# Layer 0 of a four-layer cross-attention kernel: transposed contexts by transfer, the first pair in three parts over two queues

## The chip, the core and the metric

The kernel runs on one core of a Trainium2 chip. The core has five engines with instruction streams of their own: PE (TensorE, matrix products and transposes), DVE (VectorE), ACT (ScalarE), POOL (GpSimd) and SP (SyncE, which here only issues transfers). Transfers between HBM and SBUF are carried out by 16 DMA engines; SP, ACT and POOL can issue them. The metric is the device time of one execution in microseconds (us), the median over runs.

## What is computed

The input is `x`, 16 batches of 56 tokens by 256 values, and a context `ctx_1024`, 16 batches of 1500 rows by 128 values. Four layers follow each other; each attends from the tokens of a batch to the 1500 context rows of that batch. The change touches only the first layer:

```python
def _L0_xattn_ref(hidden_states, memory, W_mem, W_gate, b_gate, norm_w):
    memory_proj = jnp.einsum('bme,de->bmd', memory, W_mem)
    scores = jnp.einsum('bnd,bmd->bnm', hidden_states, memory_proj) / jnp.sqrt(jnp.float32(D))
    attn = jax.nn.softmax(scores, axis=-1)
    memory_context = jnp.einsum('bnm,bmd->bnd', attn, memory_proj)
    gate_input = jnp.concatenate([hidden_states, memory_context], axis=-1)
    gate = jax.nn.sigmoid(jnp.einsum('bnf,df->bnd', gate_input, W_gate) + b_gate)
    fused = hidden_states + gate * memory_context
    return _rmsnorm(fused, norm_w)
```

The kernel multiplies the queries by `W_mem` first, so that scores and weighted sums are products with the context itself. Layers 1 and 3 are multi-head cross-attention with a feed-forward part, layer 2 is self-attention, cross-attention and a two-expert feed-forward part.

## The kernel before

**Tiling.** The 16 batches form four groups of four (`groups`, `gi`), and within a group two pairs, so that layer 0 runs over eight pairs, 0 to 7. The context of a batch is needed in two forms. For the weighted sums (line 610) its rows must lie on the partitions: `load_pair` (lines 506 to 518) brings it as a tile `kv` of 125 partitions by 12 x 128 values, 6144 bytes on each partition, 750 KB. For the scores (line 557) the 128 features must lie on the partitions: `turn_pair` (lines 520 to 538) makes a tile `kt` of 128 x 1500 by 12 PE transposes for each context (line 530), four into one PSUM tile, and a copy out of each PSUM tile, in turn by DVE (line 535) and ACT (line 536, recorded under line 245). The PSUM tiles of `turn()` come from a pool with two buffers. `scores_pair` (line 545) makes the scores of a pair in three columns of 500, both batches side by side, with the maxima by DVE (line 569) and the exponentials by ACT (line 576). All score products of a pair stand behind the pair's last transpose in PE's order.

**Order within layer 0.** `load_first` loads the first part of the weights, pairs 0 and 1 and the rest of the weights. `first0` turns pair 0 and makes its scores. Then `att0` runs for each group and each pair `at`: it loads pair `at + 2`, turns pair `at + 1` and makes its scores, and then transposes the weights of pair `at` (line 598) and makes its weighted sums (line 610). The hook `side()` at the head of a group finishes the group before (`post0`, lines 626 to 668) and prepares the next one (`pre0`: tokens `x` by a transfer, line 174; transposes, line 252; queries, line 498). A scheduler puts each engine's instructions into one fixed order when the kernel is built; each engine then follows its order, and an instruction that waits holds up all behind it. A transfer's issue stands in the order of its issuing engine and waits there until the tile that it fills is free.

**Buffers.** `kv` of pair n comes from the tag `kv`, `ot` or `hT` for n modulo 3 equal to 0, 1, 2, each with two buffers, so pair n + 3 reuses those of pair n and waits for pair n's weighted sums. The two `kt` of a pair come from the tags `kt` and `qa`, two buffers each.

**Queues.** The first context of a pair is loaded by SP, the second by POOL. SP's order over layer 0 is: the weights `w` (128 KB), `kv` of pairs 0 and 1, `w` (640 KB), `b_gate`, `norm_w`, the tokens of group 1, `kv` of pair 2, the tokens of groups 2 and 3, then loads for layer 1 that the scheduler put early (`Wq` 1024 KB, line 161; `WkT` and `Wv`, 512 KB each; a key mask `m32l` of 12 KB, line 143; `l2w` 256 KB; a second `Wq`), `kv` of pair 3, two more masks `m32l`, then `kv` of pairs 4 to 7. The masks have one buffer: each must have been expanded by POOL (line 147, to the tile `mkl`) before the next is loaded. POOL's order is: `kv` of pairs 0, 1 and 2, `mkl`, `kv` of pair 3, `mkl`, `kv` of pairs 4 to 7, each in its second context.

Of the kernel before, what the change touches and what calls it, by code (L numbers as in the profile page):

```python
# [9 lines left out]
F32 = mybir.dt.float32  # L10
# [10 lines left out]
B, N, M = 16, 56, 1500  # L21
D, DM = 256, 128
# [6 lines left out]
NS, SW = 3, 500  # L29
# [9 lines left out]
R = H * N  # L39
# [23 lines left out]
def tile_kernel(ctx: ExitStack, tc: tile.TileContext, a, layers=4, groups=NG):  # L63
# [3 lines left out]
    nc = tc.nc  # L67
# [3 lines left out]
    kpool = ctx.enter_context(tc.tile_pool(name="ctxp", bufs=2))  # L71
    mpool = ctx.enter_context(tc.tile_pool(name="mask", bufs=2))
    big = ctx.enter_context(tc.tile_pool(name="big", bufs=2))
# [19 lines left out]
    def turn():  # L93
        return psum(ps_t, "t")
# [149 lines left out]
    def scalar_copy(out, in_, scale=1.0):  # L244
        nc.scalar.activation(out, in_, AF.Copy, scale=scale)  # L245
# [159 lines left out]
    line, memory_w, halves_of, queries, heads_w, cross = {}, [], {}, {}, {}, {}  # L405
# [70 lines left out]
    def load_first():  # L476

        w = wpool.tile([128, 2048], F32, tag="w", name="w")
        memory_w.append(w)
        nc.sync.dma_start(w[:, :256], a["L0_w"][:, :256])  # L480
        load_pair(0)
        load_pair(1)
        nc.sync.dma_start(w[:, 256:1536], a["L0_w"][:, 256:])
        nc.sync.dma_start(w[:, 1536:1792], a["b_gate"].to_broadcast([128, D]))
        nc.sync.dma_start(w[:, 1792:], a["norm_w"].to_broadcast([128, D]))
# [19 lines left out]

    def load_pair(n):

        kvs = []
        for b, queue in ((2 * n, nc.sync), (2 * n + 1, nc.gpsimd)):

            if n % 3:
                kv = big.tile([128, 2 * R], F32, tag=("ot", "hT")[n % 3 - 1], name="kv_")
                kv = kv[:CP, : NC * DM].rearrange("p (c d) -> p c d", c=NC)
            else:
                kv = kpool.tile([CP, NC, DM], F32, tag="kv", name="kv")
            queue.dma_start(kv, a["ctx"][b])
            kvs.append(kv)
        halves_of[n] = kvs

    def turn_pair(n):  # L520
        kts = [
            kpool.tile([DM, M], F32, tag="kt", name="kt"),
            big.tile([128, 2 * R], F32, tag="qa", name="kt_")[:, :M],
        ]
        kvs = halves_of[n]
        for s in range(NS):
            for i in range(2):
                t = turn()
                for j in range(4):
                    last = nc.tensor.transpose(  # L530
                        t[:, j * CP : (j + 1) * CP], kvs[i][:, 4 * s + j, :], ident[:CP, :CP]
                    )
                dst = kts[i][:, s * SW : (s + 1) * SW]
                if (i + s) % 2:
                    nc.vector.tensor_copy(dst, t[:, :SW])
                else:
                    scalar_copy(dst, t[:, :SW])
        halves_of[n] = kts, kvs, last.ins.name

    def first0(gi, state):  # L540
        if not gi:
            turn_pair(0)
            scores_pair(0)
# [36 lines left out]
    def att0(gi, state, then, side, ends, last):  # L580
# [3 lines left out]
        for b0 in range(0, G, 2):  # L584
# [3 lines left out]
            if at + 2 < B // 2:  # L588
                load_pair(at + 2)
            if at + 1 < B // 2:  # L590
                turn_pair(at + 1)
                scores_pair(at + 1)
# [782 lines left out]
```

## Time and profile before

| | |
|---|---|
| median of 3 runs | 1768.75 us (1766.23, 1775.0, 1768.75) |
| profiled execution, its own time | 1774.53 us |
| span of the profiled execution | 1772.7 us, mean granted PE clock 0.986 |
| PE busy over the span | 1668.2 us (94%) |
| DVE, ACT, POOL busy | 1126.1, 1022.1, 112.1 us |
| moved by transfers | 106.80 MB, mean 60 GB/s |
| PE busy from 0 to 67 us | 35.9 us of 67 |
| PE busy from 67 to 165 us | 85.3 us of 98 |
| PE busy from 165 us to the end | 1547.0 us of 1607 |

The span is the time from the first to the last instruction of one profiled execution; the execution's own time is a little longer. Layer 0 takes up the first 170 us or so, where the work of layer 1 begins to mix in. In the tables of windows that follow, each row gives a stretch of the span, its length, the busy time of PE, of PE's weight loads, of DVE, ACT and POOL with their numbers of instructions, the granted clock, the mean busy share of the 16 DMA engines and what they moved in GB/s. In a timeline, a row gives the start, the length, the engine and line, and in brackets how long the engine sat idle before and what it waited for. `SPq` is the instruction stream of SP.

### The profile page before, as it was taken

What the parts mean: (1) busy time and instruction counts of PE and PEld (TensorE: products, weight loads), DVE (VectorE), ACT (ScalarE), POOL (GpSimd) and SP (SyncE); (2) the same over time, 40 slices, a digit from 0 to 9 for tenths busy, and PEclk for the clock granted to TensorE, in tenths of its full rate; (3) what the DMA queues carried; (4) which work ended last, traced back from release to release, by engine and by line L of the source; (5) the groups of instructions that cost most, each with busy time, mean ns of one, the idle gap of its engine ahead of it and who ended that gap; (6) DMA issues with size and microseconds to landing.
All of it is one profiled execution on the core that took longest, in us unless ns stands there. A gap on an engine that the chain in (4) does not pass through costs nothing.

```text
span 1772.7 us, 55493 instructions
## 1 busy us (share of the span) xinstructions
PE 1668.2 (94%) x23964; PEld 1104.3 (62%) x23964; DVE 1126.1 (64%) x2742; ACT 1022.1 (58%) x3580; POOL 112.1 (6%) x238
## 2 busy tenths in 40 slices
PE   4888999999999999999999999999999999999997
PEld 2566777776664556545665556556656777777765
DVE  2344866657765666777657776576488746666672
ACT  1443976757454446553755547457555876766663
POOL 0000000000011000110000000000000000000000
PEclk9999999999999999999999999999999999999998
DMA  6431203020030121000210002211200132212120
GB/s 175 126 109 45 77 24 108 25 89 25 14 133 28 43 97 46 21 20 20 99 69 20 20 20 99 74 38 43 99 21 16 48 119 64 76 52 89 44 68 8
DMA packets 60132, 106.80 MB, mean 60 GB/s; under 512 B 7430, under 2 KB 44950, under 8 KB 59878
## 3 DMA queue, kind: packets, MB, share of 16 engines
q1 hardware_dynamic: 58726, 97.01, 17.0%
q0 software_dynamic: 1152, 6.14, 1.4%
q8 instruction: 190, 3.11, 0.7%
q14 instruction: 64, 0.52, 0.1%
HBM read 102.23 MB, written 0.92 MB: 58 GB/s over the span
## 4 chain that ended last, share of the span: by engine, by line
PE 77%; DVE 12%; ACT 6%; DMA 3%; issue 2%; POOL 1%; SPq 0%; POOLq 0%; DVEq 0%
PE sc L339 21%; PE o L795 9%; PE mm L1166 4%; ACT p L381 4%; PE o L1133 4%; DVE p L392 4%; PE mm L858 3%; PE mm L846 3%; PE mm L831 3%; PE mm L682 3%; PE mm L1179 2%; PE t L702 2%; DVE p L344 2%; PE t L1055 2%; PE t L743 2%; PE t L751 2%
## 5 line engine op out<-in xcount | busy, mean ns | idle before, releaser
L381 ACT ACTIVATE p<-p,few 128x96 f32<-128x96 f32 (+1 forms) x1344 | 588.3, 440 | 3.8
L339 PE MATMUL sc<-kt,qa 128*32 128x375 f32 x3584 | 407.8, 486 | 5.1 <-issue 3.1
L392 DVE STREAM_TRANSPOSE p<-p 128x480 f32<-128x480 f32 (+3 forms) x319 | 316.5, 1003 | 53.0 <-ACT p L381 52.1
L344 DVE CUSTOM_DVE_ANT_0 p<-sc,no_mask 128x375 f32<-128x375 f32 x448 | 236.4, 536 | 95.1 <-PE sc L339 86.3
L381 ACT ACTIVATION_READ_ACCUMULATOR p<-p,few 128x1 f32 x1344 | 252.2, 188 | 0.0
L339 PE MATMUL sc<-ktl,qa 128*32 128x96 f32 x7168 | 200.1, 249 | 2.3 <-issue 1.6
L339 PEld LDWEIGHTS sc<-kt,qa 128*32 128x32 f32 x3584 | 126.8, 109 | 107.7 <-issue 70.1
L1133 PEld LDWEIGHTS o<-p,vc 128*32 128x32 f32 x6144 | 142.9, 110 | 75.8 <-issue 51.2
L339 PEld LDWEIGHTS sc<-ktl,qa 128*32 128x32 f32 x7168 | 157.7, 110 | 34.0 <-issue 17.3
L795 PE MATMUL o<-p,kvl 128*128 128x448 f32 x384 | 167.9, 565 | 1.2 <-DVE p L392 1.2
L1133 PE MATMUL o<-p,vc 128*32 128x64 f32 (+1 forms) x6144 | 159.7, 215 | 8.7 <-DVE p L392 7.1
L245 ACT ACTIVATE few<-t 128x14 f32<-128x14 f32 (+2 forms) x128 | 22.2, 174 | 212.7 <-PE t L373 212.7
L350 DVE TENSOR_TENSOR p<-sc,mkl 128x480 f32<-128x480 f32 (+1 forms) x192 | 113.6, 607 | 25.5 <-PE sc L339 25.3
L354 DVE TENSOR_REDUCE few<-p 128x5 f32<-128x480 f32 (+1 forms) x192 | 114.4, 612 | 2.8
L795 PEld LDWEIGHTS o<-p,kvl 128*128 128x128 f32 x384 | 67.0, 191 | 55.3 <-issue 44.7
L245 ACT ACTIVATE qa<-t 128x224 f32<-128x224 f32 (+1 forms) x96 | 38.4, 420 | 91.4 <-PE t L702 62.7
L1166 PE MATMUL mm<-xT,w 128*128 128x224 f32 (+1 forms) x384 | 81.0, 360 | 1.1 <-DVE h2T L1171 0.9
L1166 PEld LDWEIGHTS mm<-xT,w 128*128 128x128 f32 (+1 forms) x384 | 65.7, 178 | 15.6 <-DVE h2T L1171 5.3
L1055 PE MATMUL t<-l2w,kt 128*32 128x128 f32 x1536 | 60.2, 275 | 6.2 <-issue 5.8
L245 ACT ACTIVATE ot<-o 128x448 f32<-128x448 f32 x64 | 33.8, 527 | 54.0 <-PE o L795 54.0
L702 PE MATMUL t<-qT,wl 64*128 64x112 f32 x512 | 55.4, 284 | 3.2 <-DVE qa L713 2.0
L757 DVE TENSOR_TENSOR oT<-t,over 128x224 f32<-128x224 f32 x64 | 31.8, 551 | 41.3 <-PE t L751 38.2
(262 smaller groups left out, 2293.8 us busy)
## 6 DMA issues: line engine op xcount, KB each, us to landing
w<-in_L_W SPq DMA_DIRECT2D x16, 1024.0 KB
kt<-in_ctxT SPq DMA_DIRECT2D x16, 768.0 KB
w<-in_L_Wq SPq DMA_DIRECT2D x8, 1024.0 KB
w<-in_L_Wo SPq DMA_DIRECT2D x8, 1024.0 KB
ktl<-in_ctxT SPq DMA_DIRECT2D x32, 192.0 KB
kvl<-in_ctx_last SPq DMA_DIRECT2D x32, 192.0 KB
w<-in_L_v_qkv SPq DMA_DIRECT2D x4, 768.0 KB
w<-in_L_l_qkv SPq DMA_DIRECT2D x4, 768.0 KB
```

What stands on the lines that cost most here:

```text
L245: nc.scalar.activation(out, in_, AF.Copy, scale=scale)
L339: nc.tensor.matmul(sc[g * BW : (g + 1) * BW, at : at + w], q, k, start=True, stop=True, skip_group_check=True,)
L344: return nc.vector.tensor_tensor_reduce(u["p"][:, i, :w], sc[:, :w], u["mask"], 1.0, LOWEST, ALU.add, ALU.max, u["mx"][:, i : i + 1],).ins ...
L350: nc.vector.tensor_tensor(p, sc[:, : m * w].rearrange("p (i k) -> p i k", i=m), u["mask"].unsqueeze(1).to_broadcast([128, m, w]), ALU.add,)
L354: return nc.vector.tensor_reduce(u["mx"][:, i : i + m], p, AX.X, ALU.max).ins.name
L381: nc.scalar.activation(u["p"][:, i, : u["w"]], u["p"][:, i, : u["w"]], AF.Exp, bias=u["shift"][:, i : i + 1], accum_out=u["den"][:, i : i ...
L392: turned = nc.vector.transpose(blocks, blocks)
L702: nc.tensor.matmul(halves[e][:, j * TP : (j + 1) * TP], wkT[e * 64 : (e + 1) * 64, j0 + j, :], qT[e * 64 : (e + 1) * 64, j0 + j, tok], sta ...
L795: nc.tensor.matmul(o[:, : ub * BW], kv[:, j, :], p, start=start, stop=stop)
L1055: nc.tensor.matmul(p[g * BW : (g + 1) * BW, (j - j0) * DM : (j - j0 + 1) * DM], made["kt"][:, g, j * BW : (j + 1) * BW], cv, start=True, s ...
L1133: nc.tensor.matmul(o[cols, : pieces * BW], made["v"][:, j, cols], p.rearrange("p (i g) r -> p g i r", g=4)[:, g], start=start, stop=stop, ...
L1166: nc.tensor.matmul(p[:w, k * T : (k + 1) * T], wt[:, c, cols], xe[n][:, c, :], start=(c == 0), stop=(c == 1),)
```

## The change

For every pair but the first, the transposed tile of the pair's first context is loaded by SP from `ctxT`, an array with the transposed contexts that the kernel already has in HBM for later layers (128 rows of 6000 bytes, 750 KB). Only the second context of such a pair is still turned by PE: 12 transposes and 3 copies where there were 24 and 6. The tiles `kt` are now allocated in `load_pair`. The `kv` tiles are all still loaded, since the weighted sums need them. The second context of pairs 0 and 1 is loaded by ACT in place of POOL. For pair 0, each of the two contexts is loaded in three transfers of four of its twelve blocks (125 rows of 2048 bytes each).

```diff
 def load_pair(n):
     kvs = []
-    for b, queue in ((2 * n, nc.sync), (2 * n + 1, nc.gpsimd)):
+    kts = [
+        kpool.tile([DM, M], F32, tag="kt", name="kt"),
+        big.tile([128, 2 * R], F32, tag="qa", name="kt_")[:, :M],
+    ]
+    other = nc.scalar if n < 2 else nc.gpsimd
+    for b, queue in ((2 * n, nc.sync), (2 * n + 1, other)):
...
-        queue.dma_start(kv, a["ctx"][b])
+        for s in range(1 if n else NS):
+            cols = slice(None) if n else slice(4 * s, 4 * s + 4)
+            queue.dma_start(kv[:, cols], a["ctx"][b][:, cols])
         kvs.append(kv)
-    halves_of[n] = kvs
+    if n:
+        nc.sync.dma_start(kts[0], a["ctxT"][2 * n])
+    halves_of[n] = kts, kvs
 
 def turn_pair(n):
-    kts = [
-        kpool.tile([DM, M], F32, tag="kt", name="kt"),
-        big.tile([128, 2 * R], F32, tag="qa", name="kt_")[:, :M],
-    ]
-    kvs = halves_of[n]
+    kts, kvs = halves_of[n]
     for s in range(NS):
-        for i in range(2):
+        for i in range(1 if n else 0, 2):
```

## The prediction, made before the changed kernel ran

> **What bounds the kernel now.** I read the table of windows first, to find where PE is idle; then the chain of work that ended last, for what ends that idle time; then the timelines of PE, SP and POOL. Over the whole span PE is busy 94%, and from 165 us on 1547.0 us of 1607 with the DMA engines 0.17 busy. The change works before that, where PE is not the only bound.
>
> ```profile
> core 0: us, PE busy (x) PEld busy (x) DVE busy (x) ACT busy (x) POOL busy (x), PEclk, DMA share, GB/s
> 10.00:20.00 10.00, 0.00 (x0) 0.00 (x0) 0.00 (x0) 0.28 (x1) 0.00 (x0) 1.00 1.01 212
> 25.00:30.00 5.00, 5.00 (x25) 3.97 (x25) 1.44 (x3) 1.76 (x3) 0.00 (x0) 1.00 0.32 129
> ...
> 60.00:65.00 5.00, 3.66 (x51) 2.86 (x47) 0.51 (x2) 2.18 (x4) 0.00 (x0) 1.00 0.33 114
> 75.00:79.00 4.00, 3.37 (x25) 2.69 (x25) 3.07 (x6) 1.80 (x5) 0.00 (x0) 1.00 0.32 128
> ```
>
> Two things stand here. While SP's and POOL's contexts move together (10 to 20 us) all 16 DMA engines are busy, at 212 GB/s, 13 GB/s each. When little but one of SP's 125-row contexts is left (the other three rows) the share is 0.32, that is five engines of 16, at 25 GB/s each, 125 GB/s together. So a context by SP occupies five engines for 768,000 bytes / 125 GB/s = 6.1 us; POOL's contexts spread wider. I call those the five engines; my estimate is that a transfer of 128 rows (the weights, `kt`) or by POOL puts 5/16 of its bytes on them: 1.9 us for 750 KB.
>
> ```profile
> 9.33 27.36 DMA x<-in_x
> ...
> 36.74 1.01 PE mm L252 x4
> ...
> 49.91 1.12 PE o L610 x16
> 51.02 15.85 DMA kv<-in_ctx
> ...
> 67.01 0.70 PE t L530 x3
> ```
>
> The chain: PE waits for the tokens of group 1, which land at 36.7 us behind the contexts, and then for the context of pair 3, which is issued when pair 0's sums free its buffer at 51.0 and lands at 67.0 (2.2 us of PE idle).
>
> ```profile
> 121.88 3.90 PE L530 MATMUL t<-ident,kv 125*128 125x125 f32 x24
> 125.72 0.63 PE L557 MATMUL sc<-kt,l 128*64 128x500 f32 x1
> ```
>
> Turning a pair costs PE 3.84 us before its scores.
>
> ```profile
> 52.83 0.26 POOL L147 TENSOR_SCALAR mkl<-m32l 128x96 bf16<-128x96 uint8 x1 [44.90 <-DMA m32l<-in_mask_last]
> 53.35 0.57 POOL L516 DMA_DIRECT2D kv<-in_ctx  x1 [0.25 <-issue]
> 67.13 0.26 POOL L147 TENSOR_SCALAR mkl<-m32l 128x96 bf16<-128x96 uint8 x1 [13.21 <-DMA m32l<-in_mask_last]
> 67.61 0.57 POOL L516 DMA_DIRECT2D kv__509<-in_ctx  x1 [0.22 <-issue]
> 88.32 0.52 POOL L516 DMA_DIRECT2D kv__621<-in_ctx  x1 [20.15 <-PE o L610]
> ```
>
> POOL's loads stand behind its mask expansions, and those wait for masks that come through SP's queue. Pair 4's load went out at 67.6, right after a mask; PE needed it only at 88.6.
>
> **The change, part by part.**
>
> *Removed:* 12 transposes and 3 copies for each of pairs 1 to 7. In pair 4 the groups of four transposes start at 88.63, 89.15, 89.90, 90.57, 91.32, 91.89 and the scores at 92.47. With three groups the scores start about 0.6 after 89.90, 2.0 earlier; the first copy is now DVE's (0.68) and no longer ACT's (0.59): 1.9 us a pair, on PE's path. The copies gone from DVE and ACT are off the path.
>
> *Pair 0 in parts, ACT in place of POOL.* Four issues on ACT at SP's 0.28 to 0.38 us are 1.4 us between ACT's 7.1 and its next instruction at 9.92: hidden. An issue can block on a full queue (SP's third context took 11.27 us to issue at 9.86); ACT would then be free near 20, and its first copy is not needed much before. The bytes are dearer. By POOL a context took 1.9 us of the five engines; by a 125-row transfer of ACT it should take 6.1, as SP's do. No row shows an ACT transfer. The other bound is POOL's 1.9 (the tokens, below, would then land at 7.0 + 23.2 + 8.6 x 4120/3370 = 40.7); I take 6.1, since shape and source are SP's.
>
> The Trainium skill speaks against this part: in "DMA: Bandwidth & Descriptors", section "Why a DMA increments its semaphore by 16 and not by 1", a transfer of SP or ACT runs on the largest number of engines up to 16 that divides the slowest dimension of both sides, which for 125 rows is 5, while a direct copy by POOL may use all 16. By that rule the sum stands as below, with the tokens at 45.3; without it, with 40.7.
>
> *The start.* Work of the five engines up to the tokens of group 1, at 25 GB/s each: `w` 0.3, four contexts 24.6, POOL's pair 2 1.9, `kt` of pair 1 (now ahead of the tokens) 1.9, 896 KB of weights 2.3, tokens 0.6: 31.6 us. Before it was 0.3 + 2 x 6.1 + 3 x 1.9 + 2.3 + 0.6 = 21.1, and took 29.7 (7.0 to 36.7), so 8.6 were lost to sharing with the other eleven. Those now carry 2620 KB and no longer 3370, so I take 8.6 x 2620/3370 = 6.7. Tokens at 7.0 + 31.6 + 6.7 = 45.3, 8.6 later. Bounds: no loss, 38.6; the old ratio 29.7/21.1 = 1.41 on all of it, 51.6. Pair 0's own last part lands no earlier than its context did (0.3 + 12.3 + 1.9 of work, times 1.41, from 7.0: 27, against 24.4), so the parts buy nothing: PE waits at the tokens anyway. After the tokens PE has their transposes (1.0), the rest of pair 1's scores (2.2), queries (1.0) and pair 0's sums (45.13 to 51.02, 5.9), little of it overlapped: 9.9. Pair 0's sums end at 55.2, 4.2 late.
>
> *Pair 3.* Pair 2 gives back 1.9: PE is ready for pair 3 at 64.83 + 2.3 = 67.1. POOL's context, now ahead of the mask in POOL's order, goes out at 55.2 and lands 11.7 later (the median of its rows), 66.9. SP's context is no longer needed for turning, so the old wait goes; but the late start has used it up. Net at this point: 0.1 late; after pair 3's turn 1.8 early.
>
> *The masks.* All of this part is an estimate from the ratios above. In the built order SP now has `kt` of pair 3 (waits for pair 1's scores), `Wq`, pair 3's context (waits for pair 0's sums), `WkT`, `Wv`, `kt` of pair 4, and only then the first mask; `l2w`, `Wq`, pair 4's context, and then the second. Work on the five from the tokens to the first mask: pair 2's context 6.1, `kt` 1.9, tokens 1.1, `kt` 1.9, `Wq` 2.6, pair 3 6.1 + 1.9, `WkT` and `Wv` 2.6, `kt` 1.9 = 26.1. Before, from the tokens to pair 3's context, 23.7 took 30.3 us, 1.28 times. So first mask 45.3 + 33.4 = 78.7 (it was there by 52.8), pair 4 out at 79.0, landed 7.3 later (its row) at 86.3; PE is ready at 88.63 - 1.8 = 86.8: just in time. To the second mask: `l2w` 0.7, `Wq` 2.6, pair 4 6.1 + 1.9 = 11.3, times 1.28 = 14.5: 93.2. Then pair 5 by POOL, 10.0 in its row: 103.5. PE is ready at 101.65 - 1.8 - 1.9 = 97.9 and waits 5.6 us, with the end of group 0 queued behind those transposes. Pairs 6 and 7 stand behind no mask and have a whole pair's time.
>
> *Sum:* at pair 5 +1.9, then three turns of 1.9: -3.8 us. Beyond 165 us PE is the bound and keeps it. Profiled execution 1774.53 - 3.8 = 1770.7 (span 1768.9). That execution lies 5.8 above the median of the runs shown, so the forecast for the median is 1768.75 - 3.8 = 1765.
>
> **Rivals.**
>
> *The transfers keep up* (30%). For it: over the windows from 60 to 140 us the DMA engines are only 0.31 busy. Against it: the five engines' queue has some 70 us of work before the second mask. If the second mask lands by 87, pair 5 does not wait: 0.1 - 5 x 1.9 = -9.4, 1759. If the start is no later either, pair 3 is turned at 62.9 in place of 67.0: -4.1 - 9.5 = -13.6, 1755.
>
> *Slower: the mask gate on POOL* (27%). With the start's ratio 1.41 on all of it: tokens 51.6, first mask 88.4, second mask 104.3, pair 5 landed at 114.6, 13.0 after its old start, less 5.7: +7.3, 1776. It decides once the second mask lands after 97 (101.65 + 5.7 - 10.3); each microsecond more is one on the end. For it: the first window shows 13 GB/s an engine whenever all are busy. Against it: there are fewer loads by POOL at the start.
>
> *The change doesn't do what it says:* the first pair is not earlier by the parts. That is in my sum, not a case apart.
>
> **How the numbers follow.** Forecast (43%): 1765, own range 1760 to 1773. A measurement of this kernel tells about 0.5%, 8.8 us, from no change. Faster by more: nearly all of the first rival, 0.28. Slower by more: rather over half of the second, whose ratio must reach 1.46, 0.16. Else 0.56. The range reaches into both rivals, 1755 to 1778.
>
> **What would show it.** Right: 12 transposes for pairs 1 to 7 and 1.9 us before the scores; DMA share near 0.32 for most of 18 to 40 us; PE idle until the tokens at 42 to 48; POOL's mask expansions near 79 and 93, each directly ahead of a context; a PE wait at pair 5's first transposes. Wrong: tokens by 40, or no wait at pair 5 (then faster), or ACT held for more than 15 us at its issues, or a wait at pairs 6 or 7, which I exclude.

## The result and the profile after

The changed kernel takes 1763.59 us, the median of six runs (1759.62 to 1765.84); the kernel before, in six runs beside it, 1770.88 us (1766.23 to 1775.0). The ratio is 0.9967, 95% interval 0.9949 to 0.9985: faster by 0.33%, some 6 us, less than the 0.5% that the prediction took for a clear difference.

| profiled execution | before | after |
|---|---|---|
| its own time, span | 1774.53, 1772.7 us | 1765.84, 1763.9 us |
| PE busy over the span | 1668.2 us | 1659.2 us |
| PE busy from 0 to 67 us, granted clock there | 35.9 us, 0.97 | 35.6 us, 0.95 |
| PE busy from 67 to 165 us | 85.3 us | 85.0 us |
| moved by transfers, of it by ACT's queue | 106.80 MB, none | 112.16 MB, 1.54 MB |
| first scores of pairs 3, 5, 7 | 78.81, 112.06, 144.48 us | 76.86, 106.91, 136.94 us |

(The added lines shift the numbers: the turning transposes are now line 537, the scores 564, the weighted sums 617, a context's load 525, a transposed context's 528.)

The windows of the changed kernel; behind the length come the busy times of PE, its weight loads, DVE, ACT and POOL, the granted PE clock, the DMA share, and GB/s:

```profile
10.00:20.00 10.00, 3.01 (x10) 2.36 (x11) 0.00 (x0) 0.41 (x2) 0.00 (x0) 1.00 0.53 142
13.00:16.00 3.00, 0.00 (x0) 0.00 (x0) 0.00 (x0) 0.00 (x0) 0.00 (x0) 1.00 0.30 115
...
44.00:49.00 5.00, 4.83 (x14) 2.36 (x16) 1.31 (x3) 0.13 (x1) 0.00 (x0) 0.50 0.37 131
```

Where all 16 engines were busy before (share 1.01 from 10 to 20 us), they are now half busy: from 13 to 16 us three queues have contexts under way (SP's, ACT's and the rest of POOL's, which lands at 16.6), and still the share is that of five engines of 16. With SP's and ACT's alone, from 16.6 to 18.7 us, it is 0.32. The last row shows something that the prediction did not have: PE at a granted clock of 0.50.

The chain of the changed kernel (start, length, what):

```profile
6.99 25.41 DMA kv<-in_ctx
...
32.80 11.33 DMA x<-in_x
...
44.17 1.01 PE mm L252 x4
...
57.47 12.18 DMA kv<-in_ctx
...
69.79 0.51 PE t L537 x3
```

Pair 0's third part lands at 32.4 us (its whole context did at 24.4), the tokens of group 1 at 44.1 (before: 36.7). The context of pair 3 goes out at 57.5 when pair 0's sums have freed its buffer, and PE turns it at 69.8, 2.8 us later than before.

PE's timeline in the changed kernel:

```profile
37.55 0.58 PE L564 MATMUL sc<-kt,l 128*64 128x500 f32 x1
...
44.17 1.01 PE L252 MATMUL mm<-ident,x 112*128 112x112 f32 x4 [2.57 <-DMA x<-in_x]
45.11 1.10 PE L564 MATMUL sc<-kt__155,l 128*64 128x500 f32 x1
...
99.58 0.49 PE L537 MATMUL t<-ident,kv__579 125*128 125x125 f32 x3
...
118.51 1.16 PE L537 MATMUL t<-ident,kv 125*128 125x125 f32 x8
119.87 0.65 PE L537 MATMUL t<-ident,kv 125*128 125x125 f32 x4 [0.20 <-DVE kt__716 L542]
120.44 0.63 PE L564 MATMUL sc<-kt,l 128*64 128x500 f32 x1
```

The same product of scores takes 0.58 us before the wait for the tokens and 1.10 behind it: that is the half clock. Pair 5 (99.58) has no wait in brackets. Pair 6 is turned in 1.93 us (118.51 to 120.44) and no longer in 3.84.

POOL's timeline in the changed kernel:

```profile
76.29 0.27 POOL L147 TENSOR_SCALAR mkl<-m32l 128x96 bf16<-128x96 uint8 x1 [18.29 <-DMA m32l<-in_mask_last]
76.75 0.57 POOL L525 DMA_DIRECT2D kv__484<-in_ctx  x1 [0.19 <-issue]
89.80 0.27 POOL L147 TENSOR_SCALAR mkl<-m32l 128x96 bf16<-128x96 uint8 x1 [12.48 <-DMA m32l<-in_mask_last]
90.27 0.57 POOL L525 DMA_DIRECT2D kv__579<-in_ctx  x1 [0.21 <-issue]
```

Pair 4's and pair 5's loads each stand directly behind a mask expansion, as predicted; the masks are there 2.4 and 3.4 us earlier than the sum had them.

### The profile page after: what moved, and what is told of

It is laid out like the page before. It is cut to its first block, busy times and chain, and to the rows that moved or that the text cites. A ratio compares the mean times of both kernels' runs of the same rounds, so it can differ in the third digit from the quotient of the medians.

```text
span 1763.9 us, 55328 instructions
## 1 busy us (share of the span) xinstructions
PE 1659.2 (94%) x23880; PEld 1090.2 (62%) x23880; DVE 1121.6 (64%) x2735; ACT 1014.3 (58%) x3566; POOL 111.4 (6%) x236
## 2 busy tenths in 40 slices
DMA packets 61631, 112.16 MB, mean 64 GB/s; under 512 B 7534, under 2 KB 45054, under 8 KB 61378
## 3 DMA queue, kind: packets, MB, share of 16 engines
q10 hardware_dynamic: 520, 1.54, 0.3%
## 4 chain that ended last, share of the span: by engine, by line
PE 76%; DVE 12%; ACT 6%; DMA 3%; issue 2%; POOL 1%; SPq 0%; POOLq 0%; DVEq 0%
PE sc L339 21%; PE o L802 9%; ACT p L381 4%; PE mm L1173 4%; DVE p L392 4%; PE o L1140 4%; PE mm L865 3%; PE mm L853 3%; PE mm L838 3%; PE mm L689 3%; PE mm L1186 3%; PE t L709 2%; DVE p L344 2%; DMA kv<-in_ctx 2%; PE t L1062 2%; PE t L750 2%
## 5 line engine op out<-in xcount | busy, mean ns | idle before, releaser
L1062 PEld LDWEIGHTS t<-l2w,kt 128*32 128x32 f32 x1536 | 45.0, 111 | 21.5 <-issue 16.4
```

The source lines that it names most:

```text
L1062: nc.tensor.matmul(p[g * BW : (g + 1) * BW, (j - j0) * DM : (j - j0 + 1) * DM], made["kt"][:, g, j * BW : (j + 1) * BW], cv, start=True, s ...
```

## The experiments

Twelve variants ran. The kernel before ran beside each of them (medians 1767.0 to 1768.9 us; beside the changed kernel 1770.9), and each ratio is the one on record for those runs, which differs by up to 0.15% from the quotient of the medians. The last column is from each kernel's one profiled execution.

| run | median, us | ratio to before, 95% interval | mean granted clock of the runs | first scores of pair 7, us |
|---|---|---|---|---|
| before | 1767.0 to 1768.9 | 1 | 0.988 | 144.48 |
| changed kernel | 1763.6 | 0.9967 (0.9949 to 0.9985) | 0.987 | 136.94 |
| e1_kt_only | 1763.2 | 0.9978 (0.9964 to 0.9992) | 0.985 | 134.62 |
| e2_no_kt | 1776.2 | 1.0043 (1.0028 to 1.0058) | 0.987 | 147.03 |
| e3_no_parts | 1767.8 | 0.9987 (0.9968 to 1.0006) | 0.985 | 138.42 |
| e4_rows112 | 1755.1 | 0.9926 (0.9903 to 0.9948) | 0.986 | 126.15 |
| e5_rows124 | 1788.2 | 1.0114 (1.0093 to 1.0136) | 0.980 | 155.84 |
| e6_filler | 1769.1 | 1.0005 (0.9983 to 1.0026) | 0.985 | 143.09 |
| e7_whole112 | 1754.9 | 0.9931 (0.9904 to 0.9957) | 0.986 | 123.82 |
| e8_pool112 | 1750.9 | 0.9913 (0.9892 to 0.9933) | 0.988 | 121.09 |
| e9_filler_order | 1768.8 | 1.0007 (0.9991 to 1.0023) | 0.986 | 142.70 |
| e10_x_early | 1751.1 | 0.9907 (0.9891 to 0.9922) | 0.988 | 122.57 |
| e11_before112 | 1761.0 | 0.9951 (0.9938 to 0.9965) | 0.987 | 132.92 |
| e12_filler_order5 | 1761.7 | 0.9969 (0.9953 to 0.9984) | 0.989 | 133.30 |

### Which half of the change brings the gain

e1_kt_only undoes the move to ACT's queue and the parts:

```diff
-        other = nc.scalar if n < 2 else nc.gpsimd
+        other = nc.gpsimd
...
-            for s in range(1 if n else NS):
-                cols = slice(None) if n else slice(4 * s, 4 * s + 4)
-                queue.dma_start(kv[:, cols], a["ctx"][b][:, cols])
+            queue.dma_start(kv, a["ctx"][b])
```

> All second contexts go back to POOL's queue, each in one piece; only the transposed contexts on SP's queue stay from the change. In the changed kernel ACT's queue moved 1.54 MB and the tokens of group 1 landed at 44.13 us of the profiled span. Theory (the piece with ACT's queue and the three parts brings nothing, and the whole gain is the 1.9 us less of turning in each of four or five pairs): the tokens of group 1 land earlier than 44 us, near 40 to 41, and the time is 1758 to 1763 us, equal to or up to 4 us under the changed kernel's 1763.6. Rival (the gain comes from taking POOL's first loads to ACT's queue): the time goes back to before, 1769 to 1772 us.

Measured: 1763.2 us, just above the theory's range; tokens at 40.6 us. The transposed contexts alone bring all of the gain that can be told: the two ratios, 0.9978 and 0.9967, lie within each other's intervals.

e2_no_kt keeps ACT's queue and the parts and turns every context on PE again:

```diff
-        if n:
-            nc.sync.dma_start(kts[0], a["ctxT"][2 * n])
...
-            for i in range(1 if n else 0, 2):
+            for i in range(2):
```

> ACT's queue and the three parts stay; no transposed context is loaded, all are transposed on PE as before. Theory (the gain is in the turning): pairs 4 and 6 again take 3.8 us from turned to first scores instead of 1.95, and the time is 1768 to 1774 us, the same as before or a little over it. Rival (the gain comes from ACT's queue): the time stays at 1762 to 1766 us, that of the changed kernel.

Measured: 1776.2 us, 0.43% slower than before, a little more than the theory had. This half of the change costs time: the tokens land at 42.7 us and not at 36.7, and pair 0's sums end at 57.3 us and not at 51.0. In the place of pair 7's first scores the two halves add up (-9.9 us for e1, +2.6 for e2, -7.5 together). In the medians they do not (-0.22% and +0.43% against -0.33%); part of that may be the granted clock, whose mean is 0.985 in e1's runs against 0.988 before, and 0.003 of 1760 us is 5 us. Where in the span it was lost in the executions without a profile I cannot say.

e3_no_parts loads pair 0's contexts whole, and keeps ACT's queue:

> The changed kernel with the contexts of pair 0 each in one transfer; ACT's queue stays. Theory (the start is bound by how fast these transfers drain, so that the last third lands when the whole would, and the parts buy nothing): pair 0's scores begin within 1.5 us of the 34.37 us of the changed kernel, and the time is 1762 to 1766 us. Rival (the parts let PE turn pair 0 while the rest lands): pair 0's scores begin 3 us later or more, and the time is 3 us or more over the changed kernel, 1766 to 1769.

Measured: pair 0's scores at 35.79 us, 1.4 later, and the tokens 1.7 us earlier (42.5). On the place of pair 0 the theory holds: the parts gain 1.4 us there at most. The median, 1767.8 us, fell into the rival's range, but not by the rival's way: PE waits only 1.73 us for the tokens, no half clock follows (their transposes take 0.60 us), and pairs 2 and 3 run ahead of the changed kernel (pair 3's scores at 73.03 and not 76.86). Then pair 4's context goes out behind the first mask expansion at 77.43 and lands at 87.88, with PE waiting 3.22 us and at half clock behind it. What the whole kernel's time owes to the parts stays open; the intervals of the two ratios overlap.

### Five engines: the number of rows

e4_rows112 and e5_rows124 cut each context of SP and ACT by rows, the bytes unchanged; e5 has 124 where this has 112:

```diff
-                queue.dma_start(kv[:, cols], a["ctx"][b][:, cols])
+                for rows in (slice(None),) if queue is nc.gpsimd else (slice(0, 112), slice(112, CP)):
+                    queue.dma_start(kv[rows, cols], a["ctx"][b][rows, cols])
```

> The changed kernel, with each transfer of a context of 125 rows on SP's and ACT's queues made as two, of 112 and of 13 rows; the same bytes. Theory (a transfer of 125 rows on these two queues is spread over only five of the 16 DMA engines, and 112 rows would be spread over all of them, so that the start is bound by five engines and not by bytes): the DMA share between 10 and 30 us rises well over the 0.53 and 0.71 of the changed kernel, the tokens of group 1 land near 34 to 36 us instead of 44.13, and the time is 1752 to 1758 us. Rival (the start is bound by the bytes, or by the issuing of the queues, which have more to issue now): tokens no earlier than 42 us, time 1762 to 1767 us.

> As the run with 112 and 13 rows, with the same number of transfers and the same bytes, but cut into 124 rows and 1 row. Theory (what counts is how many of the 16 DMA engines a transfer's rows are spread over: five for 125 rows, sixteen for 112, and four for 124, since 124 rows fall into four equal parts and into no larger number of equal parts up to 16): stretches of the start show a DMA share of 0.25 where the changed kernel shows 0.33 (13 to 19 us), the tokens of group 1 land later than 44.13 us, at 48 us or more, and the time is 1766 to 1776 us. Rival (the gain of the cut at 112 came from having two transfers in place of one): the same gain here, tokens at 33 to 36 us and 1752 to 1758 us.

Windows of e4_rows112, and then one of e5_rows124:

```profile
10.00:20.00 10.00, 4.52 (x17) 3.12 (x16) 1.35 (x2) 0.83 (x2) 0.00 (x0) 1.00 0.93 229
20.00:30.00 10.00, 7.41 (x31) 3.79 (x30) 3.39 (x9) 1.17 (x2) 0.00 (x0) 1.00 1.00 284
```

```profile
16.00:19.00 3.00, 0.00 (x0) 0.00 (x0) 0.00 (x0) 0.00 (x0) 0.00 (x0) 1.00 0.26 98
```

With 112 rows the share from 10 to 20 us is 0.93 where it was 0.53, the tokens land at 32.6 us, earlier than the theory's 34 to 36, and the kernel takes 1755.1 us, as the theory had it. With 124 rows the share falls to 0.26, four engines of 16; the tokens are turned only at 50.2 us, behind a wait of 8.94 us for pair 1's second context, and the kernel takes 1788.2 us, worse than the theory's 1776. Two transfers in place of one are therefore not what helps: only the row count differs between these two kernels, and they lie 33 us apart. Of these, 18 are there when the tokens are turned; later in e5 PE also stands 11.78 us at pair 5, whose load by POOL went out only at 108.73 us, behind the second mask expansion.

The Trainium skill, "DMA: Bandwidth & Descriptors", section "Why a DMA increments its semaphore by 16 and not by 1", gives the rule that both runs follow: the largest number up to 16 that divides the slowest dimension of both sides, 5 for 125 rows, 4 for 124, 16 for 112. The shares 0.30, 0.26 and 0.93 bear it out.

e7_whole112 takes the parts out of e4, and e8_pool112 also gives the second contexts back to POOL, uncut:

```diff
-        other = nc.scalar if n < 2 else nc.gpsimd
+        other = nc.gpsimd
...
+            for rows in (slice(None),) if queue is nc.gpsimd else (slice(0, 112), slice(112, CP)):
+                queue.dma_start(kv[rows], a["ctx"][b][rows])
```

> The run with 112 and 13 rows, but pair 0's contexts no longer in three parts (each is 112 rows and 13 rows, whole); ACT's queue stays. Theory (parts buy nothing even when all DMA engines work, since all that is issued ahead shares the engines evenly, so that parts and wholes end together): pair 0's scores within 1.5 us of the 22.55 us of that run, time 1753 to 1757 us. Rival (with the engines all at work the parts let PE start turning early): pair 0's scores 3 us later or more, time 1757 to 1762 us.

> The run before this one, but all second contexts on POOL's queue in one piece of 125 rows, as in the kernel before; only SP's contexts are cut at 112 rows, and the transposed ones stay. Theory (POOL's transfers were spread over all engines already, so ACT's queue adds nothing once SP's are spread too): tokens of group 1 within 3 us of the 32.60 us of the run with 112 and 13 rows, time 1753 to 1758 us. Rival (ACT's queue is worth something of its own, because a POOL transfer is issued slowly or waits behind the mask): time 1758 us or more.

Measured for e7: pair 0's scores at 28.15 us, 5.6 later than with parts, so there the theory is wrong: once all engines work, parts do bring the first pair earlier. The time is the same (1754.9). PE's rows at the tokens, in e4 and then in e7, show where the gain goes:

```profile
32.60 1.01 PE L252 MATMUL mm<-ident,x 112*128 112x112 f32 x4 [5.20 <-DMA x<-in_x]
```

```profile
34.47 0.60 PE L252 MATMUL mm<-ident,x 112*128 112x112 f32 x4
```

With the parts PE stands 5.20 us until the tokens land and goes on at half clock; without them it comes to the tokens with no wait and at full clock, and pair 2's scores start at 47.22 us in place of 49.56.

Measured for e8: 1750.9 us, under the theory's range, tokens at 32.58. ACT's queue is not needed; the time without it is, if anything, lower. A window of e8:

```profile
20.00:30.00 10.00, 9.59 (x43) 5.03 (x42) 4.83 (x12) 3.29 (x5) 0.00 (x0) 1.00 1.01 265
```

PE is busy 9.59 us of these ten; in the changed kernel it was 2.91.

e11_before112 is the kernel before with nothing but SP's contexts cut at 112 rows:

> The kernel before, untouched by the change, with SP's contexts cut at 112 and 13 rows. Theory (the cut and the transposed loads each bring their own share: with them 1750.9 us, and the transposed loads save about 1.9 us in each of seven pairs on a PE that is the bound from 40 us on): 1758 to 1764 us. Rival one (the change's gain was only a way round slow transfers, and the cut alone does as well): 1749 to 1753 us. Rival two (the cut brings nothing without the change): 1766 to 1771 us.

Measured: 1761.0 us, ratio 0.9951. The cut alone brings 0.49%, the transposed contexts alone 0.22% (e1), both together 0.87% (e8). Both have a share of their own, as the theory said. On top of the cut the transposed contexts bring 0.38%, some 7 us (10 between the medians), of the 13 that seven turns of 1.9 would be.

e10_x_early loads group 1's tokens directly behind pair 0's first context, on top of e8:

```diff
         load_pair(0)
+        load_x(1)
         load_pair(1)
...
-        if gi:
+        if gi > 1:
             load_x(gi)
```

> The run with POOL's second contexts and SP's cut at 112 rows (1750.9 us, tokens of group 1 at 32.58 us with pair 0's sums behind them), with the tokens of group 1 loaded right behind pair 0's first context in place of behind pair 1's and the weights. Theory (the start still ends on these tokens, which stand behind 2.5 MB of the same queues): tokens land before 20 us, pair 0's sums end near 37 us in place of 42, and the time is 1745 to 1749 us. Rival (pair 1's and 2's contexts then come later by as much, and the start is bound by bytes): 1749 to 1753 us.

Measured: 1751.1 us, no gain over e8. The tokens are turned at 21.9 us, 10.7 earlier, but pair 0's scores start at 29.3 in place of 22.9, pair 1's at 34.8 in place of 28.8, and pair 0's sums end at 43.4. The rival holds: with all 16 engines at work (share 1.04 and 1.02 from 10 to 30 us), what is loaded earlier makes the rest later.

### The half clock and the masks

e6_filler puts eight idle transposes on PE in the wait for the tokens (the result is the same; the tokens' transposes overwrite them):

```diff
-    def to_T(xn):
+    def to_T(xn, filler=None):
         p = mm()
+        if filler is not None:
+            for _ in range(8):
+                nc.tensor.transpose(p[:, :128], filler[:, :128], ident)
...
-        p = to_T(x)
+        p = to_T(x, halves_of[0][1] if gi == 1 else None)
```

> The changed kernel with eight transposes of a tile that is already there (pair 0's weights, into the PSUM tile that the tokens' transposes overwrite) put on PE just ahead of the transposes of group 1's tokens, where it waited 2.57 us; their result is not used. In the changed kernel the granted clock falls to 0.50 from 43.7 to 50.2 us, and a product of scores takes 1.04 to 1.10 us there in place of 0.58. Theory (the half clock follows from PE standing idle in that wait): with PE busy through the wait the clock stays at 1.00, tokens to the end of pair 0's sums takes about 10 us in place of 12.95, and the time is 1759 to 1762 us. Rival (the clock falls for another reason, such as the load of the DMA engines, or the transposes delay the tokens as much as they save): half clock as before, and 1763 to 1767 us.

PE's timeline in e6_filler:

```profile
43.14 1.09 PE L252 MATMUL mm<-ident,p 128*128 128x128 f32 x8
45.29 0.60 PE L255 MATMUL mm<-ident,x 112*128 112x112 f32 x4 [1.07 <-DMA x<-in_x]
...
46.30 0.58 PE L567 MATMUL sc<-kt,l 128*64 128x500 f32 x1
...
91.97 1.27 PE L540 MATMUL t<-ident,kv__492 125*128 125x125 f32 x5 [6.49 <-DMA kv__492<-in_ctx]
```

Behind the wait the tokens' transposes take 0.60 us (1.01 in the changed kernel) and a product of scores 0.58 (1.10). From the tokens to the end of pair 0's sums it takes 9.3 us (45.29 to 54.6), not 12.95: the half clock came from PE's idle time, and it cost 3.6 us. Pair 2's scores start at 57.20, 2.5 us earlier than in the changed kernel. But the time is 1769.1 us: the last line shows PE waiting at pair 4. POOL's timeline says why:

```profile
80.75 0.26 POOL L147 TENSOR_SCALAR mkl<-m32l 128x96 bf16<-128x96 uint8 x1 [25.26 <-DMA m32l<-in_mask_last]
81.21 0.57 POOL L528 DMA_DIRECT2D kv__492<-in_ctx  x1 [0.19 <-PE o L620]
```

POOL stood 25 us for the first mask, and pair 4's load behind it lands at 91.8. In the changed kernel the same gate opened at 76.29, and PE found pair 4 there at 88.45. In e6 SP issued the mask earlier (64.41 us; 66.65 in the changed kernel), but 16.3 us passed from there to the expansion in place of 9.6. SP's built order had changed, with `WkT` ahead of pair 3's context; whether this or the earlier start made the mask late, no run shows.

e9_filler_order and e12_filler_order5 add to e6 an order on POOL, and nothing else in the source: the first expansion comes behind pair 4's load, and then behind pair 5's (5 in place of 4):

```diff
-        nc.gpsimd.tensor_scalar(mb, m32.bitcast(U8), BIG, -BIG, ALU.mult, ALU.add)
+        made = nc.gpsimd.tensor_scalar(mb, m32.bitcast(U8), BIG, -BIG, ALU.mult, ALU.add)
+        if b == 0 and 4 in loaded_at:
+            tc.add_manual_dep(made.ins, loaded_at.pop(4),
...
-                queue.dma_start(kv[:, cols], a["ctx"][b][:, cols])
+                loaded_at[n] = queue.dma_start(kv[:, cols], a["ctx"][b][:, cols]).ins.name
```

> The run with the eight idle transposes, and pair 4's POOL load ordered ahead of POOL's first mask conversion (in that run the conversion ran at 80.75 us, the load behind it was issued at 81.21 and landed at 91.83, and PE stood 10.62 us for it). Theory (the 2.5 us that the full clock gained there up to pair 2's scores were lost to this order on POOL, not to the transposes): the load goes out when its buffer comes free, near 66 to 70 us, PE waits less than 3 us at pair 4, no half clock follows there, and the time is 1756 to 1761 us. Rival (the load takes as long anyway, since the DMA engines are full from 50 to 70 us, or PE waits at pair 5 instead): 1763 us or more.

POOL's timeline in e9_filler_order, then PE's:

```profile
95.81 0.27 POOL L149 TENSOR_SCALAR mkl<-m32l 128x96 bf16<-128x96 uint8 x1 [11.75 <-DMA m32l<-in_mask_last]
96.31 0.57 POOL L538 DMA_DIRECT2D kv__587<-in_ctx  x1 [0.23 <-issue]
```

```profile
104.23 0.86 PE L550 MATMUL t<-ident,kv__587 125*128 125x125 f32 x3 [7.57 <-DMA kv__587<-in_ctx]
```

PE no longer waits at pair 4 (scores at 87.31; what it stood for in e6 was the 6.49 us of its row above, and 10.62 was the transfer's own time), but the time, 1768.8 us, is the rival's: the wait has moved to pair 5, whose load stands behind the second mask. That mask is issued only at 84.09, since the first expansion (83.80) has to free its buffer.

> The run before, with POOL's first mask conversion ordered behind pair 5's load in place of pair 4's. In that run pair 4 stood ready without a wait (first scores at 87.31 us, 3.1 us ahead of the changed kernel), but pair 5's load was held until the second conversion, 96.31 us, and pair 5's first scores came at 112.63 us, 5.7 us behind the changed kernel. Theory (the wait only moved from pair 4 to pair 5 because conversions and loads share POOL's queue, and the full clock's gain is kept once both loads are ahead of them): pair 5's load goes out near 80 us, its scores start at 101 to 104 us, pair 7's at 131 to 135 us in place of 142.7, and the time is 1756 to 1762 us. Rival (the transfers, not the order, are late, or pair 6's load is held instead): pair 7's scores at 138 us or later and 1764 us or more.

POOL's timeline in e12_filler_order5:

```profile
84.42 0.52 POOL L538 DMA_DIRECT2D kv__587<-in_ctx  x1 [18.41 <-PE o L630]
85.08 0.27 POOL L149 TENSOR_SCALAR mkl<-m32l 128x96 bf16<-128x96 uint8 x1
```

Pair 5's load goes out when its buffer is free (84.42, later than the expected 80, and early enough), its scores start at 103.18, pair 7's at 133.30, and the time is 1761.7 us, in the theory's range. The order on POOL was the cause: in the source nothing else differs between e9 and e12 (in the built order SP's issue of the second mask moved with it, behind pair 5's context, to 89.85 us). Against the changed kernel itself, 0.9969 and 0.9967, no gain in the median can be told; pair 7's scores are 3.6 us earlier.

## Why the prediction was right, and where its steps were not

*Turning, 1.9 us a pair: right.* 88.45 to 90.40 and 118.51 to 120.44, 1.95 and 1.93 us; before, 3.84. In e2, which turns both contexts again, pair 4 takes 3.83 us (91.18 to 95.01).

*ACT's queue and the parts, which bring nothing or less: right.* Tokens predicted at 45.3 us, measured 44.1; ACT was not held at its issues (its next activation started at 12.60). Five engines was the right count, shown by e4 and e5. The bound at 40.7, a cost like POOL's, was wrong for ACT. The last part was to land no earlier than its context did, and it landed at 32.4, not 27. (The 2620 and 3370 KB of the sum are whole transfers, of which the other eleven engines carry 11/16; the ratio is the same.) e2 measures the price of this half by itself: 7.6 us.

*From the tokens to the end of pair 0's sums, 9.9 us: too small.* Measured 12.95. The durations, all but that of the tokens' transposes, were taken from rows at full clock, and the wait for the tokens brought PE to half clock. e6 shows the 9.9 to be right without it (9.3).

*Pair 3, 0.1 us late: measured 2.8,* for the step before, with POOL's transfer 12.2 us against 11.7. At pair 4 PE is 0.2 us early (88.45 against 88.63) and 1.8 were predicted, so that 1.6 us of the error are left there. For the 1.1 us between the sum had no term; a likely source is the clock. In the kernel before, PE fell to half clock behind its wait for pair 3 too (from 67.2 to 70.6 us), and in the changed kernel, where it waits only 0.74 us there, it did not. The first products behind that wait, before and after:

```profile
67.50 1.71 PE L636 MATMUL mm<-l,w 128*128 128x224 f32 x4
```

```profile
70.14 0.93 PE L643 MATMUL mm<-l,w 128*128 128x224 f32 x4
```

No run tests this by itself.

*The masks and the wait of 5.6 us at pair 5: the term that failed.* The expansions were put at 78.7 and 93.2 us and came at 76.29 and 89.80. Pair 5's load then took 7.6 us and not 10.0, and landed at 97.9; PE was ready at 99.58. So the wait was 0, which the prediction itself had named as a sign of being wrong. With the 1.6 us from pair 3 that turns the predicted +1.9 at pair 5 into -2.1, 4.0 of the 5.0 us between the predicted span of 1768.9 and the measured 1763.9. The mechanism was right and only just did not bite: in e3 and e6 the first mask, in e5 and e9 the second, held a load until PE waited, from 3.22 us in e3 to 11.78 in e5. The ratio 1.28 for queues that share engines was too uncertain a number to place a gate within 2 us.

*The sum:* forecast 1765, measured 1763.59. That it came so near is in part luck. The change was forecast at -3.8 us and measured at -7.3 between the medians (some 6 by the ratio), and the forecast stood on 1768.75, the median of three runs, 2.1 us under that of the six. Two errors partly cancelled: 1.6 us too little up to pair 5, 5.6 us too much there. The three turns behind pair 5 came to -6.7 us of span (-2.1 to -8.8), 5.7 predicted.

*The rivals:* "the transfers keep up" came near in its weaker form (no wait at pair 5: -9.4 us, measured -8.8 of span), not in its stronger one, since the start was later. "The mask gate" came true in the variants alone.

## What to carry to other kernels

Look at the DMA share of a stretch in sixteenths before adding queues or parts: 0.31 is five engines, and here the row count of the transfer set it, so that cutting 125 rows into 112 and 13 alone was worth 0.49%, where the change studied brought 0.33% (the intervals overlap). Do not let loads stand behind compute on the same queue that waits for other transfers; such a gate cost PE nothing in the changed kernel and 6.49 us in e6, where the work ahead of it was 2.5 us faster. Count a wait of PE with the half clock that follows it.

## What the hardware showed unexpectedly

The best version here, transposed contexts with POOL's queue and SP's contexts cut (e8), takes 1750.9 us, 0.87% under the kernel before (interval 0.67% to 1.08%), and e10 is equal to it; both beat the changed kernel.

PE's clock fell to one half after a gap of only 2.57 us (41.6 to 44.2) in work that had itself been thin: in the one-microsecond windows from 39 to 43 us PE is busy 1.84 us of four. From such windows, the half clock lasted from 43.3 to 50.1 us in the changed kernel, 31.9 to 38.7 in e4, and 38.6 to 45.4 in e1, 6.8 us each; in e2 it was 3.4 us (43.2 to 46.6), and in the kernel before twice 3.4 us, around waits of only 2.91 us (36.5 to 39.9, the tokens) and 2.19 us (67.2 to 70.6, pair 3). The Trainium skill, "TensorE: Matmul & The Clock Gate", section "Part 1: The HAM clock gate (the "warmup" mystery)", puts the idle time that halves the clock, and the work that restores it, at about 3.4 us each. The lengths agree with one and two such spells, but the gaps of 2.19 to 2.91 us were shorter than the stated idle time. The kernels whose profile shows no such spell in the first 168 us (e8, e10, e12) run at a mean clock of 0.988 to 0.989, the one with the longest waits (e5) at 0.980; but the kernel before, with two short spells, is at 0.988 too, so that the mean does not count them. The clock column is no witness for the very start: it shows 1.00 there, while products of scores take 1.04 to 1.10 us at 34 to 36 us in the changed kernel, as at half clock.

Cut so that all 16 engines carry them, the contexts of the start moved at 229 to 284 GB/s (e4), at 14 to 18 GB/s an engine; five engines alone gave 115 GB/s, 23 each.
